# A fused attention and FFN kernel: order of the work in the last FFN block, a third buffer for u, and two normalizations moved from ScalarE to VectorE

## Chip, cores and metric

The kernel runs on one core of one Trainium2 chip. The metric is the device time of one execution in microseconds: 497.33 us is the median of 3 runs of the kernel before (497.23, 497.33, 497.87). One further execution was recorded by the profiler; it took 497.47 us.

## What is computed

The input x has 4 x 2048 tokens of 256 features. A chunked linear attention comes first, then a gated FFN; both are followed by a residual and a layer normalization without learned factors.

```python
# attention, chunks of C = 32 tokens
Q, K, V = x @ W_q.T, x @ W_k.T, x @ W_v.T
S = (Qc @ Kc.T) * mask            # mask = decay ** (i - j) for i >= j, else 0
O = S @ Vc
h = layernorm(x + sigmoid(x @ W_g.T) * O @ W_o.T + x)
# FFN, hidden size 768, integer weights times 1/127
u = silu(h @ wg.T) * (h @ wu.T)
out = layernorm(h + u @ wd.T)
```

## The kernel before, in words

The 8192 tokens are worked on in 16 blocks of 512 (TB), and each block as 4 groups of 128 tokens (NG = 4). The 768 hidden features of the FFN are 6 chunks of 128 (KH = 6). [...]an operand is split into a high part (`_hi`, a rounded fp32) and a rest (`_lo`, fp16 in the FFN), and TensorE multiplies the high parts and the rests one after the other into the same accumulator.

**One chunk of an FFN** is made by `ffn_up` (L862). TensorE computes the gate product into bank fg and the up product into bank fu, from both parts of the transposed h (L873). ScalarE takes Silu of the gate (s, L882). VectorE multiplies s and the up product to u (L893). ScalarE copies u to u_hi (L898), and GpSimd subtracts the two to u_lo (L899). Only then can the chunk go into the down product. Each engine takes its own instructions in the order in which the program writes them, wherever a call is wrapped in `in_turn` or `in_steady_turn`; this order, written out by hand, is what sets the schedule.

**When the copy is issued.** With the flag `lagging` set, `multiply` (L890) does not issue the copy and the subtraction of its chunk; it puts them into the list `late_splits`. The next `ffn_up` empties the list right after its own Silu (L883). So ScalarE takes the next chunk's Silu first and the copy after it. Without the flag the copy and the subtraction follow u at once. `held=True` makes `ffn_up` return `multiply` instead of calling it, so that other work may stand ahead of it.

**Normalizing the output.** The output tile r of a block (512 tokens) is scaled in place, group by group. `normalize` (L417, L420) does it on ScalarE with one activation of 128x256 for each group. The scale and the shift come from a short chain on GpSimd (`iterated_scale_and_shift`, L388 to L415). `up_beside` (L1206) runs one chunk of an FFN, puts the normalization of some groups between its Silu and its `multiply`, and so hides it beside TensorE.

**The end of the kernel** (from L1192) is written out separately. Blocks 14 and 15 are the last two. After the down product of block 14 (`ffn_down` at L1223), chunks 1 and 2 of block 15 follow, then the last copies that still lag, and `lagging` is switched off. Chunk 3 goes beside the normalization of groups 0 and 1 of block 14's output. Chunks 4 and 5 are each made in two halves of 256 tokens (`cols`): first both chunks for tokens 0 to 255, each beside the normalization of one further group (L1231 to L1233), then both for tokens 256 to 511 (L1234). SP stores each group of block 14's output by itself (L1201).

**The last down product** (L1288 to L1298) has one PSUM bank for each group of 128 tokens. The terms are split into `early` (the high parts and rests of chunks 0 to 3, 8 products) and `late` (those of chunks 4 and 5, 4 products). The order is

```python
for g, terms in ((0, early), (1, early), (2, early), (0, late), (1, late),
                 (3, early[:some]), (2, late), (3, early[some:] + late)):
```

**The tail** (L1326 to L1349) takes each group through: add of the residual on VectorE (L1304), statistics (L1312), their sum (L1315), root on ScalarE (L341), reciprocal on VectorE (L972), scaling, and store (L1201). Groups 0 and 2 are scaled on ScalarE (L1256, with a shift from L1264), group 1 on GpSimd and group 3 on VectorE (both L980). The root needs another function table than Silu, which ScalarE loads at L1251. Groups 0, 1 and 3 are stored from SP's queue and group 2 from ScalarE's. After that, a count of weights outside the exact range is loaded and a branch is taken or not (L1461 on); with these inputs it is not taken.

**Buffers.** u, s and r come from the pool `work`, which has two buffers for each tag. A third u must wait until the first has been read by both its readers (L898, L899). [...]

Of the kernel before, what the change touches and what calls it, by code (L numbers as in the profile page):

```python
# [47 lines left out]
F32 = mybir.dt.float32  # L48
# [4 lines left out]
ALU = mybir.AluOpType  # L53

P = 128
# [21 lines left out]
def kernel(  # L77
# [15 lines left out]
    nc = tc.nc  # L93
# [3 lines left out]
    KH = H // P  # L97
# [6 lines left out]
    work = ctx.enter_context(tc.tile_pool(name="work", bufs=2))  # L104
# [9 lines left out]
    def in_turn(ins):  # L114
        tc.keep_in_program_order(ins)

    def bank(name):
        return psum.tile([P, TB], F32, tag="ps", name=name)
# [201 lines left out]
    def in_steady_turn(ins):  # L320
        if steady:
            tc.keep_in_program_order(ins)
# [50 lines left out]
    def scale_and_shift(mv, std, kind, name):  # L373

        on_r, on_dst = kind
        scale, minus, shift = (
            small.tile([P, NG], F32, tag=tag, name=f"{tag}_{name}")
            for tag in ("scale", "minus", "shift")
        )
        in_turn(nc.vector.reciprocal(std, std))  # L380
        for t, sign in ((minus, -1.0), (scale, 1.0)):
            nc.gpsimd.tensor_scalar(t, std, sign * on_dst / on_r, None, ALU.mult)
        nc.gpsimd.tensor_tensor(shift, mv[:, :, 0], minus, ALU.mult)  # L383
        return scale, shift
# [3 lines left out]
    def iterated_scale_and_shift(mv, kind, name):  # L388
        on_r, on_dst = kind

        def column(tag):
            return small.tile([P, NG], F32, tag=tag, bufs=2, name=f"{tag}_{name}")

        def times(out, a, b):
            nc.gpsimd.tensor_tensor(out, a, b, ALU.mult)

        def line(out, a, slope, at_0):
            nc.gpsimd.tensor_scalar(out, a, slope, at_0, ALU.mult, ALU.add)

        v, y, t, minus, shift = map(  # L400
            column, ("v", "y", "t", "minus_mean", "term")
        )
        in_turn(
            nc.vector.tensor_scalar(
                v, mv[:, :, 1], 1 / on_dst**2, EPS * (on_r / on_dst) ** 2, ALU.mult, ALU.add
            )
        )
        nc.gpsimd.tensor_tensor(y, v, half, ALU.pow)
        nc.gpsimd.tensor_scalar(minus, mv[:, :, 0], -1.0, None, ALU.mult)
        times(t, y, y)  # L410
        times(t, t, v)
        line(t, t, -0.5, 1.5)
        times(y, y, t)
        times(shift, y, minus)
        return y, shift  # L415

    def normalize(r, scale, shift, groups=range(NG)):  # L417
        for g in groups:
            in_turn(
                nc.scalar.activation(  # L420
                    r[:, g, :],
                    r[:, g, :],
                    AF.Identity,
                    bias=shift[:, g : g + 1],
                    scale=scale[:, g : g + 1],
                )
            )
# [428 lines left out]
    late_splits, lagging = [], False  # L856

    def no_more_splits():
        while late_splits:
            late_splits.pop(0)()  # L860

    def ffn_up(b, hT, uT, chunks, cols=slice(0, TB), held=False):  # L862

        n = cols.stop - cols.start
        for hc in chunks:
            pg = bank(f"fg_{b}_{hc}_{cols.start}")[:, :n]
            pu = bank(f"fu_{b}_{hc}_{cols.start}")[:, :n]

            kinds = (0, 1) if hc % 2 == 0 else (1, 0)
            for kind in kinds:  # L870
                for pb, w in ((pg, fg), (pu, fu)):
                    for dc in range(KD):
                        product = nc.tensor.matmul(  # L873
                            pb,
                            lhsT=w[kind][:, dc, hc * P : (hc + 1) * P],
                            rhs=hT[kind][:, dc, cols],
                            start=(kind == kinds[0] and dc == 0),
                            stop=(kind == kinds[1] and dc == KD - 1),
                        )
                        in_turn(product)  # L880
            s = work.tile([P, n], F32, tag="s", name=f"s_{b}_{hc}")
            in_turn(nc.scalar.activation(s, pg, AF.Silu, scale=SCALE / H_UP))  # L882
            no_more_splits()  # L883
            if len(uT[0]) == hc:
                for kind, dtype, tiles in zip(("hi", "lo"), (F32R, F16), uT):
                    tiles.append(
                        acts.tile([P, TB], dtype, tag=f"u_{kind}", name=f"u_{kind}_{b}_{hc}")
                    )

            def multiply(hc=hc, pu=pu, s=s):  # L890
                u = work.tile([P, n], F32, tag="u", name=f"u_{b}_{hc}")
                in_steady_turn(
                    nc.vector.scalar_tensor_tensor(u, pu, U_UP / H_UP, s, ALU.mult, ALU.mult)  # L893
                )
                hi, lo = uT[0][hc][:, cols], uT[1][hc][:, cols]

                def split():
                    in_steady_turn(nc.scalar.copy(hi, u))  # L898
                    in_steady_turn(nc.gpsimd.tensor_tensor(lo, u, hi.bitcast(F32), ALU.subtract))  # L899

                if lagging:
                    late_splits.append(split)
                else:
                    split()

            if held:
                return multiply
            multiply()

    def early_and_late(parts, ws):  # L910
# [82 lines left out]
    hs, hTs = {}, {}  # L993
# [82 lines left out]
    scales_out = r_out = None  # L1076
# [11 lines left out]
    for b in range(NB - 2):  # L1088
        n = b + 2
# [47 lines left out]
        if not more:  # L1137
            scales_out = iterated_scale_and_shift(mv_out, of_out, f"out_{b}")
# [4 lines left out]
        r_before = r_out  # L1143
        if more:
# [24 lines left out]
            if b:  # L1169
                scales_out = scale_and_shift(mv_before, std_before, of_out, f"out_{b}")  # L1170
        else:
# [15 lines left out]
            scales_out = iterated_scale_and_shift(mv_out, of_out, f"out_{b + 1}")  # L1187
# [4 lines left out]
    last = NB - 1  # L1192
    per = NG // 2
    cols = [slice(i * per * P, (i + 1) * per * P) for i in range(2)]
    uT_last = [], []
    uT = [], []

    def store_groups(b, r, groups, eng=nc.sync):
        tokens = slice(b * TB + groups[0] * P, b * TB + (groups[-1] + 1) * P)
        dst = out[tokens, :].rearrange("(g p) d -> p g d", p=P)  # L1200
        in_turn(eng.dma_start(dst, r[:, groups[0] : groups[-1] + 1, :]))  # L1201

    def up(b, uT, *chunks):
        ffn_up(b, hTs[b], uT, range(*chunks))

    def up_beside(b, uT, hc, r, groups, cols=slice(0, TB)):  # L1206

        multiply = ffn_up(b, hTs[b], uT, range(hc, hc + 1), cols, held=True)
        normalize(r, *scales_out, groups)
        multiply()  # L1210

    lagging = True
# [10 lines left out]
    r_before, mv_before, _ = ffn_down(last - 1, uT, hs[last - 1], chunkwise=True)  # L1223
    scales_out = iterated_scale_and_shift(mv_before, of_out, f"out_{last - 1}")
    up(last, uT_last, 1, KH - 3)
    no_more_splits()
    lagging = False
    up_beside(last, uT_last, KH - 3, r_before, range(0, per))
    for g in range(per):
        store_groups(last - 1, r_before, [g])  # L1230
    for i in range(per):  # L1231
        up_beside(last, uT_last, KH - 2 + i, r_before, [per + i], cols[0])
        store_groups(last - 1, r_before, [per + i])  # L1233
    ffn_up(last, hTs[last], uT_last, range(KH - 2, KH), cols[1])  # L1234
    steady = False

    def loaded(count, engines):
# [32 lines left out]
    banks = [bank(f"fdn_{last}_{g}")[:, :D] for g in range(NG)]  # L1270

    early, late = early_and_late(uT_last, [chunked(w) for w in fd])
    some = len(early) // 2

    def down_products(g, terms):
        for part, w in terms:
# [11 lines left out]
    for g, terms in (  # L1288
        (0, early),
        (1, early),  # L1290
        (2, early),
        (0, late),
        (1, late),
        (3, early[:some]),
        (2, late),
        (3, early[some:] + late),
    ):
        down_products(g, terms)  # L1298
    mvs = [no_moments(f"f{last}_{g}") for g in range(NG)]
# [2 lines left out]
    def add(g):  # L1302
        in_turn(
            nc.vector.scalar_tensor_tensor(  # L1304
                r[:, g, :], banks[g], SCALE**2 / U_UP, hs[last][:, g, :], ALU.mult, ALU.add
            )
        )
# [3 lines left out]
    def stats_of(g):  # L1311
        in_turn(nc.vector.bn_stats(stats[g], r[:, g, :]))  # L1312

    def moments_of(g):
        in_turn(nc.vector.bn_aggr(mvs[g][:, g, :], stats[g]))  # L1315
        stds[g] = root(mvs[g], f"f{last}_{g}", groups=[g], order=in_turn)
# [11 lines left out]
    add(1)  # L1328
    moments_of(0)
    stats_of(1)  # L1330
    add(2)
    moments_of(1)
    inverse_of(0)
    stats_of(2)
    by_scalar(r, 0, stds[0], term_of(0))
    store_groups(last, r, [0])
    add(3)
    moments_of(2)
    inverse_of(1)
    scaled(r, 1, mvs[1], stds[1], nc.gpsimd)  # L1340
    store_groups(last, r, [1])
    stats_of(3)
    moments_of(3)
    inverse_of(2)
# [190 lines left out]
```

## Time and profile before

| | |
|---|---|
| median of 3 runs | 497.33 us |
| profiled execution | 497.47 us |
| its span on the core | 495.8 us |
| first product of the last down product | 484.03 us into the span |
| last product issued, ends | 489.97, 490.25 us |
| last u_lo ready | 489.01 us |
| VectorE's last scaling starts | 492.11 us |
| last store issued, landed | 492.80, about 494.8 us |

A row of the timeline gives the start in the span and the length (us), the engine, the line of the kernel, the operation, the tile written and the tiles read, the shape, and the number of merged instructions (x2). What stands in brackets is the engine's idle time ahead of it and the instruction that the profile takes to have ended it. PE is TensorE (PEld its weight loads), DVE VectorE, ACT ScalarE, POOL GpSimd, SPq SP's queue. In the list of waits the numbers are the total in us, the count, and the longest. In the chain of waits, each row is the start, the share of the chain in us, and what the chain runs through.

### The profile page before, as it was taken

What the parts mean: (1) busy time and instruction counts of PE and PEld (TensorE: products, weight loads), DVE (VectorE), ACT (ScalarE), POOL (GpSimd) and SP (SyncE); (2) the same over time, 40 slices, a digit from 0 to 9 for tenths busy, and PEclk for the clock granted to TensorE, in tenths of its full rate; (3) what the DMA queues carried; (4) which work ended last, traced back from release to release, by engine and by line L of the source; (5) the groups of instructions that cost most, each with busy time, mean ns of one, the idle gap of its engine ahead of it and who ended that gap; (6) DMA issues with size and microseconds to landing.
All of it is one profiled execution on the core that took longest, in us unless ns stands there. A gap on an engine that the chain in (4) does not pass through costs nothing.

```text
span 495.8 us, 12306 instructions
## 1 busy us (share of the span) xinstructions
PE 486.9 (98%) x4760; PEld 382.5 (77%) x4760; DVE 305.1 (62%) x754; ACT 375.4 (76%) x701; POOL 291.1 (59%) x324
## 2 busy tenths in 40 slices
PE   9999999999999999999999999999999999999995
PEld 5787777787977778787787978778787777967674
DVE  4576778474764847557474764847557474766555
ACT  4877697688868778787788868778787787756945
POOL 3835655655745656475655745656475555458664
PEclk9999999999999999999999999999999999999998
DMA  8820213113222231223213222231222211113101
GB/s 261 247 89 7 87 41 88 38 44 81 92 65 65 75 98 44 74 63 93 73 44 84 88 67 63 87 85 44 78 68 84 74 44 42 46 28 102 40 25 66
DMA packets 43324, 37.00 MB, mean 75 GB/s; under 512 B 4864, under 2 KB 39168, under 8 KB 43264
## 3 DMA queue, kind: packets, MB, share of 16 engines
q1 hardware_dynamic: 42144, 35.28, 23.9%
q10 hardware_dynamic: 1120, 0.92, 0.6%
q8 instruction: 38, 0.62, 0.5%
q14 instruction: 22, 0.18, 0.1%
HBM read 20.45 MB, written 8.39 MB: 58 GB/s over the span
## 4 chain that ended last, share of the span: by engine, by line
PE 86%; DVE 5%; ACT 4%; issue 2%; POOL 1%; DVEq 0%; ACTq 0%; POOLq 0%
PE fg L873 15%; PE fu L873 14%; PE fdn L730 13%; PE p_y L486 9%; PE p_g L486 8%; PE p_v L508 8%; PE p_o L508 8%; PE po L684 3%; PE ps L648 2%; PE fdn L947 2%; DVE u L893 1%; ACT s L882 1%; PE pi L193 1%; DVE st_a L332 1%; PE pv L614 1%
## 5 line engine op out<-in xcount | busy, mean ns | idle before, releaser
L899 POOL TENSOR_TENSOR u_lo<-u,u_hi 128x512 f16<-128x512 f32 (+1 forms) x98 | 128.6, 1314 | 86.0 <-ACT u_hi L898 85.3
L893 DVE SCALAR_TENSOR_TENSOR u<-fu,s 128x512 f32<-128x512 f32 (+1 forms) x98 | 66.5, 679 | 106.6 <-ACT s L882 84.0
L898 ACT CAST u_hi<-u 128x512 fp32r<-128x512 f32 (+1 forms) x98 | 59.9, 611 | 64.1 <-DVE u L893 64.0
L873 PE MATMUL fg<-hT_hi,fg_hi 128*128 128x512 f32 (+1 forms) x196 | 71.2, 444 | 0.0
L882 ACT ACTIVATE s<-fg 128x512 f32<-128x512 f32 (+1 forms) x98 | 57.0, 582 | 8.1 <-PE fg L873 8.0
L873 PE MATMUL fu<-hT_hi,fu_hi 128*128 128x512 f32 (+1 forms) x196 | 60.6, 390 | 0.0
L873 PE MATMUL fg<-hT_lo,fg_lo 128*128 128x512 f16 (+1 forms) x196 | 58.1, 378 | 0.0
L873 PE MATMUL fu<-hT_lo,fu_lo 128*128 128x512 f16 (+1 forms) x196 | 57.4, 375 | 0.0
L467 POOL TENSOR_TENSOR go_lo<-goT,go_hi 128x512 fp32r<-128x512 f32 x30 | 37.9, 1285 | 26.7 <-ACT go_hi L466 26.7
L850 POOL TENSOR_TENSOR hT_lo<-hT,hT_hi 128x512 f16<-128x512 f32 x28 | 35.4, 1287 | 23.8 <-ACT hT_hi L849 23.8
L467 POOL TENSOR_TENSOR x_lo<-xT,x_hi 128x512 fp32r<-128x512 f32 x30 | 37.9, 1284 | 14.5 <-ACT x_hi L466 14.5
L730 PE MATMUL fdn<-fd_hi,u_hi 128*128 128x256 f32 x312 | 44.6, 285 | 0.0
L873 PEld LDWEIGHTS fu<-hT_hi,fu_hi 128*128 128x128 f32 x196 | 36.5, 188 | 8.4
L784 DVE TENSOR_TENSOR h<-p_o,x 128x512 f32<-128x512 f32 x30 | 19.3, 686 | 37.4 <-PE p_o L508 35.6
L873 PEld LDWEIGHTS fg<-hT_hi,fg_hi 128*128 128x128 f32 x196 | 34.7, 189 | 9.1
L730 PEld LDWEIGHTS fdn<-fd_hi,u_hi 128*128 128x128 f32 x312 | 38.9, 188 | 0.3
L420 ACT ACTIVATE h<-h,shift_h,scale_h 128x256 f32<-128x256 f32 x52 | 27.0, 590 | 15.9 <-POOL shift_h L383 15.9
L730 PE MATMUL fdn<-fd_lo,u_lo 128*128 128x256 f16 x312 | 38.6, 273 | 0.0
L873 PEld LDWEIGHTS <-fu_lo 128*128 128x128 f16 x196 | 19.2, 98 | 22.2
L730 PEld LDWEIGHTS <-u_lo 128*128 128x128 f16 x312 | 28.4, 98 | 3.9
L873 PEld LDWEIGHTS <-fg_lo 128*128 128x128 f16 x196 | 14.1, 98 | 21.1 <-issue 13.0
L703 DVE SCALAR_TENSOR_TENSOR goT<-sg,po 128x512 f32<-128x512 f32 (+1 forms) x34 | 20.7, 652 | 15.2 <-PE po L684 15.1
(174 smaller groups left out, 1052.9 us busy)
## 6 DMA issues: line engine op xcount, KB each, us to landing
x<-in_x_dram SPq DMA_DIRECT2D x16, 512.0 KB, 4.0
xT<-in_xT_dram SPq DMA_DIRECT2D x15, 512.0 KB, 3.9
hT<-sq SPq DMA_DIRECT2D x224, 32.0 KB, 1.9
out_dram<-r SPq DMA_DIRECT2D x13, 512.0 KB, 3.1
out_dram<-r SPq DMA_DIRECT2D x7, 128.0 KB, 1.7
fg_int<-in_ffn_gT_dram SPq DMA_DIRECT2D x3, 256.0 KB, 7.9
fu_int<-in_ffn_uT_dram SPq DMA_DIRECT2D x3, 256.0 KB, 7.1
fd_int<-in_ffn_dT_dram SPq DMA_DIRECT2D x3, 256.0 KB, 5.9
```

The source lines that it names most:

```text
L420: nc.scalar.activation(r[:, g, :], r[:, g, :], AF.Identity, bias=shift[:, g : g + 1], scale=scale[:, g : g + 1],)
L467: in_turn(nc.gpsimd.tensor_tensor(lo[:, k, :], t[:, k, :], whole, ALU.subtract))
L486: nc.tensor.matmul(pb, lhsT=a[kind][:, k, i * P : (i + 1) * P], rhs=b[kind][:, k, :], start=kind + k == 0, stop=True, skip_group_check=True,)
L508: nc.tensor.matmul(pb[:, j * D : (j + 1) * D], lhsT=b[kind][:, k, g * P : (g + 1) * P], rhs=a[kind][:, k, :], start=kind + k + j == 0, sto ...
L703: nc.vector.scalar_tensor_tensor(by_pairs(goT)[:, n, r, :], by_pairs(sg)[:, n, r, :], 1.0, po[:, n, :], ALU.add, ALU.mult,)
L730: product = nc.tensor.matmul(pb[:, j * D : (j + 1) * D], lhsT=part[:, g * P : (g + 1) * P], rhs=w, start=(i == 0), stop=(i == len(terms) - 1),
L850: nc.gpsimd.tensor_tensor(in_order[1], whole, in_order[0].bitcast(F32), ALU.subtract)
L873: product = nc.tensor.matmul(pb, lhsT=w[kind][:, dc, hc * P : (hc + 1) * P], rhs=hT[kind][:, dc, cols], start=(kind == kinds[0] and dc == ...
L882: in_turn(nc.scalar.activation(s, pg, AF.Silu, scale=SCALE / H_UP))
L893: nc.vector.scalar_tensor_tensor(u, pu, U_UP / H_UP, s, ALU.mult, ALU.mult)
L898: in_steady_turn(nc.scalar.copy(hi, u))
L899: in_steady_turn(nc.gpsimd.tensor_tensor(lo, u, hi.bitcast(F32), ALU.subtract))
```

## The change

- `lagging` stays on through the whole up part of block 15, and the list is emptied only after its last chunk. So from chunk 2 on, each copy of u and the subtraction behind it are issued after the next Silu.
- u has three buffers instead of two, in all blocks.
- The normalization of groups 2 and 3 of block 14's output goes from ScalarE to VectorE, as one `tensor_scalar` with the scale and the shift as [P, 1] operands, issued behind u of the first half of chunk 4 and of chunk 5.
- In the last down product the late terms of groups 0 and 1 come ahead of the early terms of group 2, and group 3's terms are no longer split in two.
- In the tail VectorE's order changes: the sums of the statistics of group 1 go ahead of the add of group 2, and the add of group 3 goes behind the sums of group 2 and the reciprocal of group 1. ScalarE's order in the tail is unchanged.

The instructions of TensorE, GpSimd and SP stay in number; ScalarE has two fewer and VectorE two more. In the blocks ahead of the last, only the third buffer differs.

```diff
             def multiply(hc=hc, pu=pu, s=s):
-                u = work.tile([P, n], F32, tag="u", name=f"u_{b}_{hc}")
+                u = work.tile([P, n], F32, tag="u", bufs=3, name=f"u_{b}_{hc}")
...
     up(last, uT_last, 1, KH - 3)
-    no_more_splits()
-    lagging = False
     up_beside(last, uT_last, KH - 3, r_before, range(0, per))
     for g in range(per):
         store_groups(last - 1, r_before, [g])
     for i in range(per):
-        up_beside(last, uT_last, KH - 2 + i, r_before, [per + i], cols[0])
-        store_groups(last - 1, r_before, [per + i])
+        ffn_up(last, hTs[last], uT_last, range(KH - 2 + i, KH - 1 + i), cols[0])
+        g = per + i
+        in_turn(
+            nc.vector.tensor_scalar(
+                r_before[:, g, :],
+                r_before[:, g, :],
+                scales_out[0][:, g : g + 1],
+                scales_out[1][:, g : g + 1],
+                ALU.mult,
+                ALU.add,
+            )
+        )
+        store_groups(last - 1, r_before, [g])
     ffn_up(last, hTs[last], uT_last, range(KH - 2, KH), cols[1])
+    no_more_splits()
+    lagging = False
...
     for g, terms in (
         (0, early),
         (1, early),
-        (2, early),
         (0, late),
         (1, late),
-        (3, early[:some]),
+        (2, early),
         (2, late),
-        (3, early[some:] + late),
+        (3, early),
+        (3, late),
     ):
...
     add(1)
     moments_of(0)
     stats_of(1)
+    moments_of(1)
     add(2)
-    moments_of(1)
+    stats_of(2)
     inverse_of(0)
-    stats_of(2)
     by_scalar(r, 0, stds[0], term_of(0))
     store_groups(last, r, [0])
-    add(3)
     moments_of(2)
     inverse_of(1)
     scaled(r, 1, mvs[1], stds[1], nc.gpsimd)
     store_groups(last, r, [1])
+    add(3)
     stats_of(3)
```

More of the change, by code (lines that the diff above doesn't have):

```diff
@@ L1272 @@
     early, late = early_and_late(uT_last, [chunked(w) for w in fd])
-    some = len(early) // 2
     def down_products(g, terms):
```

## Prediction

> **What bounds the kernel now.** I read the page's busy shares, then TensorE's waits, then the chain of waits and the timeline of the last 16 us.
>
> ```profile
> PE 486.9 (98%) x4760; PEld 382.5 (77%) x4760; DVE 305.1 (62%) x754; ACT 375.4 (76%) x701; POOL 291.1 (59%) x324
> ```
>
> TensorE is busy 98% of the span, and its waits come to 3.4 us in all. Nothing in this change removes a product, so only two places can give time: TensorE's waits near the end, and the tail after its last product. Its waits between 480 and 490 us:
>
> ```profile
> PEld L1277 <- POOL u_lo L899: 0.5, 1, 0.5
> PE fdn L1277 <- POOL u_lo L899: 0.3, 1, 0.3
> ```
>
> One wait: weight loads stop for 0.5 us because the last u_lo (GpSimd's rest of u) is late. The timeline shows why:
>
> ```profile
> 480.59 2.53 POOL L899 TENSOR_TENSOR u_lo<-u,u_hi 128x512 f16<-128x512 f32 x2
> 481.91 0.69 DVE L893 SCALAR_TENSOR_TENSOR u<-fu,s 128x512 f32<-128x512 f32 x1 [2.13 <-ACT r L420]
> 483.33 1.98 POOL L899 TENSOR_TENSOR u_lo<-u,u_hi 128x512 f16<-128x512 f32 x2 [0.20 <-ACT u_hi L898]
> 485.80 0.74 POOL L899 TENSOR_TENSOR u_lo<-u,u_hi 128x256 f16<-128x256 f32 x1 [0.49 <-ACT u_hi L898]
> 487.04 0.73 POOL L899 TENSOR_TENSOR u_lo<-u,u_hi 128x256 f16<-128x256 f32 x1 [0.50 <-ACT u_hi L898]
> 488.28 0.73 POOL L899 TENSOR_TENSOR u_lo<-u,u_hi 128x256 f16<-128x256 f32 x1 [0.51 <-ACT u_hi L898]
> ```
>
> u of chunk 3 starts at 481.91. The page names ACT's r, but with two buffers u_3 takes that of u_1, which the first u_lo reads until 480.59 + 2.53/2 = 481.86: that is the real releaser. After it GpSimd idles about 0.5 us before each of the last three pieces, waiting for ScalarE: a round of Silu, u, copy, plus a normalization, takes ScalarE 1.23 us.
>
> The chain that ended last then runs:
>
> ```profile
> 487.79 0.41 ACT u_hi L898
> 488.20 0.02 issue
> 488.22 1.28 ACT L1251
> 489.50 0.01 issue
> 489.51 0.20 ACT table L1251
> 489.71 0.19 ACT rstd_f L341
> ```
>
> The table load stands behind ScalarE's last copy. From the root the chain goes over VectorE's queue (reciprocal, statistics of group 2, shift) into the add of group 3, and to the last store:
>
> ```profile
> 490.45 0.42 DVE L1304 SCALAR_TENSOR_TENSOR r<-fdn,h 128x256 f32<-128x256 f32 x1
> 491.11 1.23 POOL L980 TENSOR_SCALAR r<-r,mv_f,rstd_f 128x256 f32<-128x256 f32 x1 [2.10 <-DVE rstd_f L972]
> 492.11 0.41 DVE L980 TENSOR_SCALAR r<-r,mv_f,rstd_f 128x256 f32<-128x256 f32 x1
> 492.37 0.33 SPq L1201 DMA_DIRECT2D out_dram<-r  x1
> 492.80 0.38 SPq L1201 DMA_DIRECT2D out_dram<-r  x1
> ```
>
> Group 3 is ready at 492.11 + 0.41 = 492.52, but its store goes out at 492.80: SP is still issuing group 1's, which waited for GpSimd until 492.34. The last store takes 2.0 us to land (494.8), and 1.0 us of closing work ends the span at 495.8.
>
> **What the Trainium skill says.** "SBUF — State Buffer", section "Who interferes with whom": GpSimd shares one pair of ports with VectorE; a VectorE tensor_scalar in a two-port mode and a GpSimd instruction exclude each other, and the later one stops until the first is through. The trace agrees for a form without [P, 1] operands:
>
> ```profile
> 443.93 2.53 POOL L467 TENSOR_TENSOR go_lo<-goT,go_hi 128x512 fp32r<-128x512 f32 x2
> 445.51 0.97 DVE L404 TENSOR_SCALAR v_out<-mv_f 128x4 f32<-128x4 f32 x1
> 460.58 0.17 DVE L404 TENSOR_SCALAR v_out<-mv_f 128x4 f32<-128x4 f32 x1
> ```
>
> The same four columns took 0.97 us beside a GpSimd product, ending with it, and 0.17 us alone. "VectorE: DVE Perf Modes", section "Mode 2×_2P", says that a one-source fp32 instruction in SBUF may enter that mode. Whether the moved normalizations do, no row settles: the 0.41 us at 492.11 lies beside GpSimd's 1.23 us, so it may be a short instruction that waited or a long one that did not. "ScalarE: Activation LUTs", section "What ACT_TABLE_LOAD costs", gives 1283 ns; the trace has 1.28.
>
> **The change part by part.** Latencies from the trace: ScalarE to VectorE 0.08, back 0.04, ScalarE to GpSimd 0.08, product to VectorE 0.04 us.
>
> *Three buffers for u.* u_3 no longer waits for the first u_lo. In the 14 blocks ahead its start is set by the Silu anyway, and TensorE waits for none of it: nothing there. In the last one a buffer returns after three: u of chunk 4, second half, needs the u_lo of chunk 3.
>
> *Copies behind the next Silu, two normalizations on VectorE.* Two activations of 0.59 us leave ScalarE. Its order becomes s_3, copy 2, two normalizations, s_4, copy 3, s_5, copy 4, s_4', copy 5, s_5', copy 4', copy 5' (' is the second half). With s_3 at 480.17 (0.1 after fg_3) and ScalarE's own steps (0.49 after a long Silu, 0.53 after a long copy or a normalization, 0.28 and 0.31 for halves): copy 2 480.66, normalizations 481.19 and 481.68, s_4 482.17, copy 3 482.45, s_5 482.98, copy 4 483.26, s_4' 483.57, copy 5 483.90, s_5' 484.21. u_3 is ready by 481.53. Now GpSimd is the bound and runs without gaps: u_lo 3 at 483.15, then 4, 5, 4', 5' from 484.40 by 0.73 each, ending 485.13, 485.86, 486.59, 487.32 (before: the last at 489.01). u_4' waits for u_lo 3 (484.42) and u_5' for u_lo 4 (485.13); copies 4' and 5' follow at 484.94 and 485.65, in time. The table load moves to 486.1, from 488.2, so it is ready at 487.6.
>
> *VectorE's added work* is 2 x 0.41 = 0.82 us at most, in gaps of about 0.8 us that it has between two u's. Queued behind them are u_5 and u_4'; who waits for those is copy 5, then u_lo 5. Unknown is the port. Lower bound: no lock, nothing. Upper bound: the first waits until u_lo 2 ends (483.12), the second until u_lo 3 ends, and each delays GpSimd by 0.2 to 0.3: u_lo 5 ends at 486.3 to 486.45. The stores of groups 2 and 3 of r leave SP by 485, clear of the tail.
>
> *Order of the products.* Eight early products take 0.92 us, four late ones 0.47 (rows of L1277). From 484.03: early 0 to 484.85, early 1 to 485.78, late 0, late 1 to 486.72, early 2 to 487.65, late 2 to 488.12, early 3, late 3 to 489.52, and 0.24 until the last result: 489.76. Before it was 490.25, so 0.49 goes. The new danger is late 0, which begins 1.75 us after the first product instead of 2.67: its last weight is asked for at 486.15, when u_lo 5 has been there for 0.29 us. With the lock at its upper bound TensorE waits 0.15 to 0.3 there. I take 0.1.
>
> *VectorE's tail.* Adds 0 to 2 come at 486.53, 487.32 and 488.40, set by TensorE; statistics 2 at 488.84, reciprocal 0, shift 0, moments 2 and reciprocal 1 (its root done at 488.7) by 489.68. So add 3 is set by the last product at 489.80, with 0.1 for the wait 489.90: 0.55 earlier than 490.45. Behind it runs the same chain of 2.07 us, less 0.03 for moments and a reciprocal that now lie ahead: group 3 ready at 491.94. GpSimd's group 1 starts with reciprocal 1 near 489.8 and ends by 491.1, so its store is out of SP by 491.45, and the last one leaves at once, at 491.96 instead of 492.80: 0.84. Two stores overlap at the end instead of three. Lone ones landed in 1.7 us, the last of three in 2.0: I take 1.85, worth 0.15 (0 to 0.3).
>
> **Sum**: 0.49 (stall) + 0.16 (the add no longer held by the table) + 0.03 + 0.26 (SP's queue) + 0.15 (landing) - 0.1 (lock) = 1.0 us. The profiled execution took 497.47 us around a span of 495.8; the median is 497.33. So the span becomes 494.8, and the median 496.3.
>
> **Rivals.** *Half of it*: end of work isn't the last landing but the other engines' closing, or the landing stays at 2.0 and the lock takes 0.3. Against it: SP waits for out_dram at the very end (0.6 us). Gain 0.3 to 0.75, time 496.8. *Slower*: the lock starves the first moved normalization. VectorE asks while GpSimd runs u_lo 2, and GpSimd, always with a next instruction ready, keeps the ports through u_lo 3 and 4, to 485.13. Then u_5 is at 485.4, copy 5 at 485.85, u_lo 5 ends at 487.03, and late 0 stops TensorE for 0.9 us plus what a blocked GpSimd row adds (L899 has rows of 1.62 beside 1.28, so 0.34), 1.25. That turns the gain of 1.0 + 0.1 into a loss of 0.15: 497.5. It decides from a stall of 1.1 us on. Against it: at 445.51 VectorE got through as soon as one row ended. *The change doesn't do what it says*: GpSimd stays late because copy 3 isn't earlier (482.45 against 482.63), so that late 0, put forward, just takes over the stall; about 0.4 of the gain goes, 496.7, within the half case.
>
> **Chances.** A difference within 0.2% (1.0 us) is about what a measurement of this kernel can't tell from none. Forecast (gain 0.75 to 1.5) 0.70; half (with the third rival) 0.25; slower 0.05. The forecast's centre lies on the 0.2% line; gains can exceed it by 0.1 (no lock), 0.15 (landing at 1.7) and 0.1 (a scaling of group 3 no longer beside GpSimd), so of its 0.70 I put 0.52 above; of the slower rival's 0.05, 0.02 lies beyond 0.2% on its side. Faster 0.52, same 0.46, slower 0.02. The range holds the forecast with these bounds and most of the half case: 495.8 to 497.1.
>
> **What would show it.** Right: no TensorE wait at the last products, u_lo rows end to end from 480.6 to about 487.4, the table load near 486.1, add 3 some 0.05 behind the last product, last two SP stores over 0.5 us apart. The lock shows as moved normalizations longer than 0.41 us and u_lo rows above 1.3 (0.75 for halves). Wrong: a new TensorE wait at late 0, or a span that ends over 1.1 us after the last landing.

## The result, and the profile after

| | before | after |
|---|---|---|
| median of 22 runs each | 497.64 us | 496.99 us (496.19 to 497.70) |
| ratio, 95% interval | | 0.9986 (0.9980 to 0.9992) |
| profiled execution | 497.47 us | 497.36 us |
| its span | 495.85 us | 495.81 us |
| first product of the last down product, into the span | 484.03 us | 484.85 us |
| from there to the end of the span | 11.82 us | 10.96 us |

The kernel became 0.65 us faster by the medians, 0.4 to 1.0 us by the interval. The forecast was 1.0 us. The gain, 0.14%, is below the 0.2% at which the prediction drew its line, and clear of zero.

The two spans are equal all the same. The whole list of TensorE's waits in the changed kernel says why:

```profile
PE pi L193 <- PEq L1530: 1.0, 1, 1.0
PE p_y L486 <- ACT p_y L527: 1.0, 1, 1.0
PE fdn L947 <- POOL u_lo L899: 0.7, 1, 0.7
PE pv L614 <- DMA wv<-in_w_vT_dram: 0.5, 1, 0.5
PE p_v L508 <- ACT p_v L527: 0.2, 1, 0.2
PE pt L803 <- ACT h L420: 0.2, 1, 0.2
```

The wait of L1277 on u_lo is gone, as forecast. A wait for the weight wv is new, at the very start. In TensorE's timeline, this is the first product with wv, before:

```profile
8.32 1.89 PE L614 MATMUL pv<-wv,xT 128*128 128x256 f32 x8
```

and after:

```profile
9.01 1.99 PE L614 MATMUL pv<-wv,xT 128*128 128x256 f32 x8 [0.49 <-DMA wv<-in_w_vT_dram]
```

The row begins 0.69 us later in this one execution, 0.49 us of it spent waiting for this load. All later rows of TensorE run about 0.8 us behind those of before, up to the last down product. The change doesn't touch the start: in the 13 profiles of this study the row began at 8.15 to 9.29 us, with no relation to the edits. So whole spans can't be compared here to a few tenths, and I read everything from the first product of the last down product, 484.03 before and 484.85 after. The expectations below took the spans to a tenth of a microsecond and so speak of 11.77 and 10.95 for this stretch; the tables have it to the hundredth.

The part up to there, GpSimd and VectorE in the changed kernel:

```profile
481.42 6.73 POOL L899 TENSOR_TENSOR u_lo<-u,u_hi 128x512 f16<-128x512 f32 x7
...
481.68 0.69 DVE L893 SCALAR_TENSOR_TENSOR u<-fu,s 128x512 f32<-128x512 f32 x1 [1.07 <-ACT s L882]
...
483.79 0.40 DVE L1233 TENSOR_SCALAR r<-r,y_out,term_out 128x256 f32<-128x256 f32 x1
...
484.58 0.91 DVE L1233 TENSOR_SCALAR r<-r,y_out,term_out 128x256 f32<-128x256 f32 x1
```

All seven u_lo run end to end. u_3 waits for its Silu and no longer for GpSimd. The second moved normalization takes 0.91 us.

The chain of waits in the last stretch now goes through products, not through ScalarE:

```profile
485.01 5.57 PE fdn L1287 x48
...
490.61 0.43 DVE r L1314
```

The tail:

```profile
490.18 0.39 PE L1287 MATMUL fdn<-fd_lo,u_lo 128*128 128x256 f16 x2
490.61 0.42 DVE L1314 SCALAR_TENSOR_TENSOR r<-fdn,h 128x256 f32<-128x256 f32 x1
490.66 1.24 POOL L980 TENSOR_SCALAR r<-r,mv_f,rstd_f 128x256 f32<-128x256 f32 x1 [2.51 <-DVE rstd_f L972]
492.27 0.41 DVE L980 TENSOR_SCALAR r<-r,mv_f,rstd_f 128x256 f32<-128x256 f32 x1
492.67 0.38 ACTq L1201 DMA_DIRECT2D out_dram<-r  x1
```

and SP's issues of groups 1 and 3:

```profile
491.92 0.33 SPq L1201 DMA_DIRECT2D out_dram<-r  x1
492.71 0.33 SPq L1201 DMA_DIRECT2D out_dram<-r  x1
```

The add of group 3 follows the last product by 0.04 us (490.57 to 490.61). SP has long issued group 1 when group 3 is ready at 492.68, so the last store leaves at once. From the first product of the last down product, that is 7.86 us, against 8.77 before: 0.91 earlier. Of this 0.86 reaches the end of the span.

### The profile page after: what moved, and what is told of

Its sections match the earlier page's. It is cut to its first block, busy times and chain, and to the rows that moved or that the text cites. A ratio compares the mean times of both kernels' runs of the same rounds, so it can differ in the third digit from the quotient of the medians.

```text
span 495.8 us, 12306 instructions
## 1 busy us (share of the span) xinstructions
PE 487.0 (98%) x4760; PEld 382.4 (77%) x4760; DVE 306.7 (62%) x756; ACT 374.2 (75%) x699; POOL 291.3 (59%) x324
## 4 chain that ended last, share of the span: by engine, by line
PE 87%; DVE 5%; ACT 3%; issue 1%; DMA 1%; POOL 1%; ACTq 0%; DVEq 0%; POOLq 0%
PE fg L873 15%; PE fu L873 15%; PE fdn L730 13%; PE p_y L486 9%; PE p_g L486 8%; PE p_v L508 8%; PE p_o L508 8%; PE po L684 3%; PE ps L648 2%; PE fdn L947 2%; DMA wv<-in_w_vT_dram 1%; PE fdn L1287 1%; DVE u L893 1%; DVE st_a L332 1%; PE pv L614 1%
```

## The experiments

All times are from the first product of the last down product in the profiled execution, in us. The ratio is to the kernel before.

| kernel | ratio, 95% interval | last product done | add of group 3 | last store issued | end |
|---|---|---|---|---|---|
| before | 1 | 6.22 | 6.42 | 8.77 | 11.82 |
| changed | 0.9986 (0.9980 to 0.9992) | 5.72 | 5.76 | 7.86 | 10.96 |
| e1, two buffers | 0.9986 (0.9978 to 0.9993) | 5.90 | 5.94 | 8.05 | 11.17 |
| e2, old products | 0.9989 (0.9981 to 0.9997) | 5.71 | 6.44 | 8.53 | 11.64 |
| e3, old tail | 0.9984 (0.9977 to 0.9991) | 5.72 | 5.76 | 8.11 | 11.16 |
| e4, normalizations on ScalarE | 0.9987 (0.9979 to 0.9995) | 5.71 | 5.76 | 7.86 | 10.96 |
| e5, before + products | 1.0013 (1.0005 to 1.0020) | 6.69 | 6.73 | 9.09 | 12.13 |
| e6, before + lagging copies | 0.9996 (0.9988 to 1.0004) | 5.72 | 5.92 | 8.26 | 11.30 |
| e7, e4 with two buffers | 0.9991 (0.9983 to 1.0000) | 5.90 | 5.94 | 8.05 | 11.15 |
| e8, group 2 on VectorE | 0.9986 (0.9979 to 0.9994) | 5.71 | 5.75 | 7.90 | 10.93 |
| e9, other form of the normalizations | one run | 5.72 | 5.76 | 7.86 | 10.96 |
| e10, e8 + early count | 1.0002 (0.9993 to 1.0010) | 5.71 | 5.75 | 7.90 | 11.54 |
| e11, early count | 1.0005 (0.9995 to 1.0015) | 5.72 | 5.76 | 7.86 | 12.01 |

The intervals, about 0.4 us to either side, don't separate most of these from the changed kernel. So what follows on the parts rests on the columns to their right, each from a single execution; kernels that should agree there (changed, e4, e9) agree to 0.01.

**e1: the third buffer undone**

```diff
-                u = work.tile([P, n], F32, tag="u", bufs=3, name=f"u_{b}_{hc}")
+                u = work.tile([P, n], F32, tag="u", name=f"u_{b}_{hc}")
```

> The changed kernel with u back in two buffers. Measure: from the first product of the last down product to the end of the span (11.77 us in the profiled execution before, 10.95 after), since that stretch holds all that the change touches. Main theory: u of chunk 4 and 5 come later, and u_5 (first half) stands behind a normalization that waits for GpSimd's ports, so that the late products of group 0 meet u_lo 5 about 0.2 us late: 11.15, ratio to before 0.999. Rival A: the third buffer is the core of the change, since u_3 waited 1.2 us for it; without it the gain is lost: 11.6 or more. Rival B: the buffer does nothing, as the copies are behind the next Silu anyway: 10.95.

Measured: 11.17, as the main theory had it, with this wait of the weight loads, and these rows on GpSimd and VectorE:

```profile
PEld L1287 <- POOL u_lo L899: 0.2, 1, 0.2
```

```profile
483.37 2.03 POOL L899 TENSOR_TENSOR u_lo<-u,u_hi 128x512 f16<-128x512 f32 x2 [0.20 <-ACT u_hi L898]
485.65 1.48 POOL L899 TENSOR_TENSOR u_lo<-u,u_hi 128x256 f16<-128x256 f32 x2 [0.26 <-ACT u_hi L898]
...
483.54 1.26 DVE L1233 TENSOR_SCALAR r<-r,y_out,term_out 128x256 f32<-128x256 f32 x1
484.72 0.41 DVE L893 SCALAR_TENSOR_TENSOR u<-fu,s 128x256 f32<-128x256 f32 x1
```

The normalization took 1.26 us beside GpSimd, u_5 stood behind it, and GpSimd idled ahead of u_lo 5. That looked like the port lock as the cause; e7 tests it. Rival A falls: 0.65 of the 0.86 us stay. u_3 again starts 2.12 us ahead of the first product, as before, and not 3.18 as with three buffers. The normalization on ScalarE ends only after that start here, so it was the buffer that held u_3 before, as the prediction read it, and not the r that the page named.

**e2: the old order of the products** (the changed tail stays)

```diff
-        (0, late), (1, late), (2, early), (2, late), (3, early), (3, late),
+        (2, early), (0, late), (1, late), (3, early[:some]), (2, late), (3, early[some:] + late),
```

> The changed kernel with the order of the last products as before. Same stretch. Main theory: no TensorE wait, as the last u_lo is there by 2.5 us after the first product and is asked for at 4.2; TensorE ends at the same time, but the adds of groups 0 and 1 come about 1 us later, so the reciprocals of groups 0 and 1, which stand ahead of the add of group 3 on VectorE, hold that add by about 0.3 us: 11.25. Rival: the order of the products is what removes the stall: a TensorE wait of 0.3 to 0.5 comes back, and 11.4.

Measured: 11.64, without a TensorE wait. The mechanism of the main theory holds, at 0.69 us and not 0.3. VectorE's rows:

```profile
489.29 0.39 DVE L1315 SCALAR_TENSOR_TENSOR r<-fdn,h 128x256 f32<-128x256 f32 x1
...
490.45 0.13 DVE L972 RECIPROCAL rstd_f<-rstd_f 128x1 f32<-128x1 f32 x1
490.50 0.40 DVE L1315 SCALAR_TENSOR_TENSOR r<-fdn,h 128x256 f32<-128x256 f32 x1
```

The add of group 2 comes at 489.29 (5.23), the add of group 3 at 490.50 (6.44), behind reciprocal 1, though its bank was full at 5.71. The add of group 2 comes directly behind the sums of group 1's statistics (489.19), which the new tail order puts ahead of it.

**e3: VectorE's old order in the tail** (the new products stay)

```diff
-    moments_of(1)
     add(2)
-    stats_of(2)
-    inverse_of(0)
+    moments_of(1)
+    inverse_of(0)
+    stats_of(2)
...
+    add(3)
     moments_of(2)
     inverse_of(1)
...
-    add(3)
```

> The changed kernel with VectorE's order in the tail as before. Same stretch. Main theory: the add of group 3 still follows the last product, but the reciprocal of group 1 comes behind it, GpSimd's scaling of group 1 ends about 0.5 us later, and its store stands ahead of the last one in SP's queue again: last store issued 0.15 to 0.2 us later, three stores landing together: 11.15 to 11.3. Rival: the order on VectorE is free since the chain behind the last add sets the end: 10.95.

Measured: 11.16. The add of group 3 stays at 5.76 and VectorE's last scaling at 7.42. But reciprocal 1 comes later, GpSimd starts to scale group 1 at 6.43 instead of 5.81, its store goes out at 7.69 instead of 7.07, and the last at 8.11: 0.25 in SP's queue. So the new tail order is worth its 0.20 us through GpSimd and that queue; VectorE's own last row doesn't move.

**e4: the normalizations back on ScalarE**

```diff
-        ffn_up(last, hTs[last], uT_last, range(KH - 2 + i, KH - 1 + i), cols[0])
-        g = per + i
-        in_turn(nc.vector.tensor_scalar(r_before[:, g, :], ...))
-        store_groups(last - 1, r_before, [g])
+        up_beside(last, uT_last, KH - 2 + i, r_before, [per + i], cols[0])
+        store_groups(last - 1, r_before, [per + i])
```

> The changed kernel with the normalizations of groups 2 and 3 of block 14's output back on ScalarE, each behind the Silu and the lagging copy. Same stretch. Main theory, worked out from the rows of the profile after: GpSimd remains the bound up to chunk 4, copy 5 comes about 0.7 us later, u_lo 5 of the first half is ready at 2.08 us after the first product and is asked for at 2.15: no TensorE wait, or below 0.1, so 10.95 to 11.05. Rival: the 1.18 us that go back to ScalarE delay the late products of group 0 by 0.3 to 0.6 us: 11.3 to 11.5.

Measured: 10.96 and no TensorE wait. The move to VectorE is worth nothing here: with the copies behind the Silus and three buffers, ScalarE has room for the 1.2 us, and GpSimd is the bound with it too.

**e5: the kernel before with the new products alone**

```diff
-        (2, early), (0, late), (1, late), (3, early[:some]), (2, late), (3, early[some:] + late),
+        (0, late), (1, late), (2, early), (2, late), (3, early), (3, late),
```

> The kernel before with only the new order of the last products. Stretch from the first product of the last down product to the end of the span (11.77 before, 10.95 with the whole change). Main theory: the order is of use only when the u_lo are early. Here late 0 asks for u_lo 5 at 2.1 us after the first product, and it is ready at 2.5; late 2 then asks at 4.45 and the last u_lo comes at 5.0: two TensorE waits of 0.4 and 0.6 in place of one of 0.5, the last product 0.5 later, the end about 0.4 later: 12.15. Rival: the new order alone is worth something, since the adds of groups 0 and 1 come earlier: 11.5 or less.

Measured: 12.13, two waits in place of one. The profile's list for the stretch:

```profile
PE fdn L1277 <- POOL u_lo L899: 0.5, 2, 0.3
```

Without early rests the order of products is a loss of 0.31 us. The timed ratio agrees (1.0013).

**e6: the kernel before with the lagging copies alone**

```diff
     up(last, uT_last, 1, KH - 3)
-    no_more_splits()
-    lagging = False
...
     ffn_up(last, hTs[last], uT_last, range(KH - 2, KH), cols[1])
+    no_more_splits()
+    lagging = False
```

> The kernel before with only the copies of u behind the next Silu to the end (two buffers, normalizations on ScalarE, old products, old tail). Same stretch. Main theory: this alone takes away the TensorE wait (0.5 us) and the table load's place in the chain, but not the hold of the last store by SP's queue: 11.2 to 11.3, that is about 0.5 of the 0.82 us. Rival: with ScalarE still carrying the two normalizations GpSimd stays late and nothing changes: 11.7.

Measured: 11.30, no TensorE wait, last product at 5.72 as in the changed kernel. Moving the copies alone takes all of TensorE's 0.50 us, with two buffers. The timed ratio, 0.9996, doesn't show a gain by itself; its interval holds both this 0.51 us and none. The add of group 3 still comes 0.20 behind the last product, and the last store leaves 0.28 after its data (8.26 against 7.98): SP's queue.

Here the table load starts at 487.12, about 1 us earlier in the stretch than before, and is out of the way. VectorE's rows up to the add of group 3:

```profile
487.12 1.28 ACT L1251 ACT_TABLE_LOAD   x1
...
488.92 0.41 DVE L1304 SCALAR_TENSOR_TENSOR r<-fdn,h 128x256 f32<-128x256 f32 x1
489.24 0.17 DVE L1315 BATCH_NORM_AGGREGATE mv_f<-st_last 128x2 f32<-128x6 f32 x1
489.33 0.13 DVE L972 RECIPROCAL rstd_f<-rstd_f 128x1 f32<-128x1 f32 x1
489.38 0.41 DVE L1312 BATCH_NORM_STATS2 st_last<-r 128x6 f32<-128x256 f32 x1
489.70 0.20 DVE L1264 TENSOR_SCALAR shift<-mv_f,rstd_f 128x1 f32<-128x1 f32 x1
489.82 0.41 DVE L1304 SCALAR_TENSOR_TENSOR r<-fdn,h 128x256 f32<-128x256 f32 x1
```

From the add of group 2 on they follow without a gap. So it is VectorE's own queue that holds the add of group 3, with the table loaded early too. In e3, with the same old tail order but the new products, the add of group 2 comes at 4.37 instead of 5.01, and the add of group 3 at 0.04 behind the last product. It is the order of the products that frees it.

**e7: e4 with two buffers**

```diff
-                u = work.tile([P, n], F32, tag="u", bufs=3, name=f"u_{b}_{hc}")
+                u = work.tile([P, n], F32, tag="u", name=f"u_{b}_{hc}")
```

> The changed kernel with both the third buffer and the move of the normalizations undone; the lagging copies, the product order and the tail stay. Same stretch. Theory after the first four runs: the third buffer is needed only because the normalizations stand on VectorE and wait there for GpSimd's ports; without them two buffers do: 10.95 to 11.05, no TensorE wait. Rival: two buffers cost their 0.2 us by themselves (u_5 waits for u_lo 3): 11.15 and a weight-load wait of 0.2.

Measured: 11.15 with the same wait of 0.2 and the same last product (5.90) as e1. My theory that the third buffer is needed only because of VectorE's wait for the ports falls. VectorE's u rows show what it is:

```profile
484.14 0.42 DVE L893 SCALAR_TENSOR_TENSOR u<-fu,s 128x256 f32<-128x256 f32 x1 [0.56 <-POOL u_lo L899]
485.64 0.42 DVE L893 SCALAR_TENSOR_TENSOR u<-fu,s 128x256 f32<-128x256 f32 x1 [1.07 <-POOL u_lo L899]
486.33 0.42 DVE L893 SCALAR_TENSOR_TENSOR u<-fu,s 128x256 f32<-128x256 f32 x1 [0.26 <-POOL u_lo L899]
```

With two buffers each u waits for GpSimd to be through with the second u before it. Then the copy has to be made before GpSimd can go on, and GpSimd idles 0.29 us. That costs 0.18 us at the last product with or without a normalization on VectorE. e6 had two buffers and no wait; its old order of products asks for u_lo 5 later. So the third buffer pays because the new order asks earlier.

**e8: group 2 scaled on VectorE**

```diff
-    by_scalar(r, 2, stds[2], term_of(2))
+    scaled(r, 2, mvs[2], stds[2])
```

> The changed kernel with group 2 of the last output scaled on VectorE too, between the reciprocals of groups 2 and 3, where it is idle, instead of on ScalarE with a shift. Same stretch. Theory: in the changed kernel the two last stores go out within 0.04 us of each other and the later one lands 2.2 us after issue; here group 2's goes 0.4 us earlier, the last one 0.05 later but alone, landing in 1.7 to 1.8: 10.6 to 10.7. Rival: the end is set by the engines' closing work and not by the landing: 11.0.

Measured: 10.93. Group 2's store left 0.44 us earlier (7.38) and landed in 1.8 us. The last landing moved from 10.02 to 9.61, the end by only 0.03: the rival holds. It is seen in what SP waits for at the end, before:

```profile
SPq L1531 <- DMA out_dram<-r: 0.6, 1, 0.6
SPq L1531 <- remote: 0.3, 1, 0.3
```

after:

```profile
SPq L1541 <- remote: 0.6, 1, 0.6
SPq L1541 <- DMA out_dram<-r: 0.2, 1, 0.2
```

and in e8:

```profile
SPq L1541 <- remote: 0.9, 1, 0.9
```

SP's wait for the stores shrinks from 0.6 to 0.2 to none, and what the page calls remote takes its place. I read it as the other engines' closing: SP's wait ends 0.12 us behind the start of GpSimd's last semaphore row of the branch in all three traces (9.54 and 9.66 before, 8.88 and 9.01 changed, 9.18 and 9.30 in e8). In e8 this row itself comes 0.30 later than in the changed kernel, above all because the load of the count takes longer there. GpSimd's load, changed and e8:

```profile
L1250 POOLq TENSOR_LOAD <-n_wide x1: 488/488/488, 492.8 to 492.8; - x1
```

```profile
L1250 POOLq TENSOR_LOAD <-n_wide x1: 743/743/743, 492.2 to 492.2; - x1
```

So e8 moved two things at once, the landing forward and the closing back. What the earlier landing is worth alone it doesn't show, nor why the load took 0.74 instead of 0.49 us.

**e9: the moved normalizations as subtract, then multiply**

```diff
-                scales_out[0][:, g : g + 1],
-                scales_out[1][:, g : g + 1],
-                ALU.mult,
-                ALU.add,
+                mv_before[:, g, 0:1],
+                scales_out[0][:, g : g + 1],
+                ALU.subtract,
+                ALU.mult,
```

> The changed kernel with the two moved normalizations written as subtract the mean, then multiply (the form that scales group 3 at the end), instead of multiply, then add. Looked at: the length of the two rows on VectorE, 0.40 and 0.91 us in the changed kernel, the second ending 0.16 us after GpSimd's row beside it. If every VectorE tensor_scalar of this shape contends with GpSimd, the second is again 0.8 to 0.9. If the form decides, both are 0.41, as the scaling at the end, and GpSimd's rows stay at 1.28. The stretch to the end stays at 10.95 either way.

Measured, on VectorE:

```profile
482.98 0.40 DVE L1233 TENSOR_SCALAR r<-r,mv_f,y_out 128x256 f32<-128x256 f32 x1
...
483.77 0.92 DVE L1233 TENSOR_SCALAR r<-r,mv_f,y_out 128x256 f32<-128x256 f32 x1
```

0.40 and 0.92, as with the other form: the form doesn't decide.

**e10 and e11: the count's cast ahead of the tail**

```diff
+    n_wide = const.tile([1, 1], I32, tag="n_wide", name="n_wide")
+    in_turn(nc.vector.tensor_copy(n_wide, count))
     add(0)
     stats_of(0)
...
-    n_wide = const.tile([1, 1], I32, tag="n_wide", name="n_wide")
-    in_turn(nc.vector.tensor_copy(n_wide, count))
```

> As the run with group 2 on VectorE, and the cast of the count of wide weights, which the other engines load before they close, moved from behind the last scaling to ahead of the first add of the tail. Same stretch (10.95 in the changed kernel, 10.97 with group 2 on VectorE alone). Theory: with group 2 on VectorE the end is no longer the last landing but the engines' closing, which starts with the load of the count 0.2 us behind the cast; with the cast early GpSimd, TensorE and ScalarE close sooner and the landing of the last store at about 9.65 sets the end: 10.6 to 10.75. Rival: closing starts when the last engine is through anyway (VectorE's own load stands behind the last scaling): 10.95.

> The changed kernel with only the cast of the count moved ahead of the tail's first add. Same stretch. Theory: here the two last stores land at 10.0, about when the engines' closing ends, so that taking the closing away gives little: 10.85 to 10.95, with SP's last wait on the store. Rival: the closing alone set the end: 10.7.

Measured: 11.54 and 12.01, a loss of 0.61 and 1.05 against e8 and the changed kernel. Neither theory nor rival had that. Up to the last store's start nothing differs (7.90 and 7.86). Then, in e11, SP's last issue and the landings:

```profile
491.89 0.96 SPq L1201 DMA_DIRECT2D out_dram<-r  x1
```

```profile
out_dram<-r SPq DMA_DIRECT2D x3, 128.0 KB, 3.1
out_dram<-r ACTq DMA_DIRECT2D x1, 128.0 KB, 2.5
```

The issue takes 0.96 us instead of 0.33, and SP's stores land in 3.1 us (median) instead of 1.7. TensorE and GpSimd had loaded the count, branched and begun to close while stores were still under way. The trace shows one thing that came with it. In before, changed, e8, e10 and e11 a DMA packet of 16 KB, of the kind instruction, starts 1.07 to 1.08 us behind TensorE's last branch. In the changed kernel TensorE branches at 8.82 and the packet starts at 9.90, when the packets of all stores are through. In e11 TensorE branches at 5.91, the packet starts at 6.99, in the middle of the stores, and takes 1.42 us; one of 8 KB follows at 8.01. The DMA queues of e11 from 6.97 to 8.27:

```profile
q1 hardware_dynamic: 239, 0.23, 50.7%
q8 instruction: 1, 0.02, 6.8%
q14 instruction: 1, 0.01, 3.5%
```

The same stretch of the changed kernel has packets of q1 alone. Each store's landing is recorded in 16 parts. Of the first store's, 15 landed at 7.75 to 7.93 in e11, as all 16 do in the changed kernel, and one at 9.65. That instruction packets hold up single parts of the stores fits this, but no run isolates it, and why SP's issue takes 0.96 us stays open. No run gave a version clearly better than the changed kernel.

## Why the prediction was right, point by point

*TensorE's wait, 0.49*: right. Last product 6.22 to 5.72, 0.50. e6 shows that the lagging copies remove it, and e5 that the new products alone don't.

*The add no longer held by the table load, 0.16*: the size came true (0.20 behind the last product before, 0.04 after), the reason did not. The table load did move as forecast, to 2.14 us after the first product of this stretch (forecast 2.07, 486.1 less 484.03). But e6 has it early too, and the add is still 0.20 behind. What freed it is the order of the products, through the earlier add of group 2 (e6 and e3). That the number fits is luck: any cause that left the add behind the last product would have given it.

*VectorE's chain behind it, 0.03*: nothing. From the start of the add to the end of the scaling it took 2.07 us before and after.

*SP's queue, 0.26*: right, 0.25. e3 gives it back.

*Two normalizations off ScalarE*: worth nothing (e4). The prediction had read ScalarE's round of 1.23 us as Silu, u, copy and a normalization. The rows of before show a round of the same length without one:

```profile
485.63 0.38 ACT L882 ACTIVATE s<-fg 128x256 f32<-128x256 f32 x1
486.56 0.41 ACT L898 CAST u_hi<-u 128x256 fp32r<-128x256 f32 x1 [0.55 <-DVE u L893]
486.87 0.38 ACT L882 ACTIVATE s<-fg 128x256 f32<-128x256 f32 x1
```

From one Silu to the next it is 1.24 us, and ScalarE idles for 0.55 of it, waiting for u. The round was set by the chain Silu, u, copy, with the copy ahead of the next Silu; the normalization fitted into the idle time.

*The port lock, -0.1*: the mechanism is there, the cost isn't. The moved normalizations took 0.40 and 0.91 us, against 0.41 with GpSimd idle, so the second waited some 0.5 us. The GpSimd row that both of them touched took 1.39 us, against 1.30 for the same row in e4, where no normalization runs beside it. All this stayed inside the slack, and TensorE waited for none of it.

*Landing, +0.15*: the step that failed. The last store left 0.91 us earlier, the end came 0.86 earlier: from the last store's issue to the end it took 3.05 us before and 3.10 after. SP's last store still took 2.0 us, though fewer stores were under way with it. Group 2's, which left at nearly the same time from ScalarE's queue, took 2.2 instead of 2.0 and is now the last to land: at 10.02, against 10.81 for SP's last store before, 0.79 earlier. The term was to give 0.15 and took 0.12; 0.07 came back because the end followed the last landing after 0.94 instead of 1.01 us. That the landing stays at 2.0 was in the rival "half of it". So was the closing of the engines, which e8 shows to be next in line.

*The rivals*: half of the gain hidden, not in the profile, except for that term. Slower by starved normalizations, no: each of the two ended 0.24 and 0.15 us behind the GpSimd row that was running when it began, though GpSimd had the next one ready. Late 0 taking over the stall, no: none is left.

So the sum in the profile is 0.50 + 0.16 + 0.25 - 0.05 = 0.86 us against 0.99 forecast. The medians give 0.65, with an interval of 0.4 to 1.0 that holds both. By the medians alone the gain lies in the range of "half of it" (0.3 to 0.75) and below that of the forecast (0.75 to 1.5); it is the profile that speaks for the forecast.

What the forecast took as one package is in truth unequal. The lagging copies give 0.51 by themselves (e6). With them the new products add 0.15 (e3 against e6; these two differ also in the buffers and the normalizations, but TensorE's last product is at 5.72 in both), and the new tail order 0.20 more. Each of these two needs what stands ahead of it: the products alone cost 0.31 (e5), and the new tail with the old products is 0.34 slower than both old (e2 against e6). The third buffer saves 0.2 once the new products are there, and the move to VectorE nothing.

## What to carry to other kernels

When ScalarE makes something that a slower engine must finish before TensorE can go on, look at what stands ahead of it in ScalarE's queue: here a Silu that was ready went behind a copy that wasn't, and turning the two around was most of the gain in the profile. An order that uses results sooner pays only when they come sooner; on its own it cost 0.31 us here. When two things stand ahead of an instruction, here a table load and VectorE's own queue, taking one away shows which of them held it. When the last transfer moves forward, ask what else ends the program before crediting its landing.

## What the runs showed of the hardware that I had not expected

- A VectorE tensor_scalar with two [P, 1] operands, fp32, 128x256, contends with GpSimd: 0.91 us (changed) and 1.26 us (e1) beside a GpSimd row, each ending about 0.15 us behind that row, against 0.41 in the tail with GpSimd idle (492.27). "SBUF — State Buffer", section "Who interferes with whom", describes the lock; the trace of before had left open whether this form takes part.
- The first microseconds differ from one execution to the next and shift all that follows by up to 1.1 us (first product with wv at 8.15 to 9.29 in 13 profiles). In the changed kernel's profile 0.49 us of it is a wait for a load; in the latest, e7, TensorE waits for no load there, and its products ahead of it (L572) take 4.48 us instead of 3.60 before. The cause is open.
- An earlier cast of one number made SP's last three stores land in 3.1 us (median) instead of 1.7 (e11). A 16 KB instruction packet, which starts 1.07 to 1.08 us behind TensorE's last branch in five profiles, then falls among the stores; that it is the cause is not shown.
